# Twelve array splits per pair of heads instead of eighteen, and output sums shared by two pairs

## The chip, the cores and the metric

The kernel runs on one core of a Trainium2 chip. The metric is the device time of one execution in microseconds (us), the median of several runs. The core has TensorE (PE for its matmuls, PEld for its weight loads), VectorE (DVE), ScalarE (ACT), GpSimd (POOL), and SyncE (SP), which here issues most transfers. TensorE's results go to PSUM, which attention uses as eight banks of 128 partitions x 512 float32: four for scores, projections, values and outputs, and four for the products with the values.

TensorE's array can be used whole (128*128 in the profile's rows) or in parts that work side by side: 64*128 is two row groups, 32*64 is four row groups by two column groups. A stretch of matmuls of one such form is called a *split* below.

## The reference, cut to what matters

Four batches of 1024 tokens of width 256 go through causal attention with 16 heads of 64 (rotary positions on queries and keys), a residual sum and a layer norm, then through 16 experts of which each token takes its best 3, and another residual sum and norm. All is float32.

```python
proj = x @ W_in.T + b_in                      # q, k, v of 16 heads
q = _rope(q, sin, cos); k = _rope(k, sin, cos)
att = softmax(where(tril, q @ k.T / 8, -inf))
y = (att @ v) per head
x = layernorm(x + (y @ W_out.T + b_out))
gate = softmax(x @ gate); the best 3, made to sum to 1
x = layernorm(x + sum over the 3 of gate_e * (relu(x @ W1_e + b1_e) @ W2_e + b2_e))
```

## The kernel before, in words

**Pairs of heads.** Attention goes through 32 pairs (4 batches x 8 pairs of heads; two heads fill 128 partitions). The numbers of heads and keys are the same in each pair, and causality makes the work a triangle: a chunk is 128 queries, and query chunk c meets c+1 blocks of 128 keys, c from 7 down to 0.

**The steps of a pair n**, with their functions and lines:
- `project` (L265): queries and keys for 512 tokens at a time (`pp`, L282, 128*128). VectorE reads the bank once (bias, times sine, L287), ScalarE once (bias, L293, `raw`). Four DMAs swap halves of `raw` into `swp` (L305), and `rotate` (L309) on GpSimd multiplies by the cosine and adds (L321, L326). Queries have a lower and an upper half (g = 0 and 1). A pair's projections are made during the pair before.
- `values` (L328): v for two pairs at once (`vv`, L335), copied out by ScalarE (L340), stored to DRAM and read back in another layout by `spread` (L352) into `vr`.
- `scores` (L364): matmuls of 64*128, the two heads side by side (`s`, L385). VectorE takes each bank with a custom reduction (mask, scale, running minimum, L393) and writes `p`; ScalarE then takes exponentials with row sums (L408). `divide` (L419): a reciprocal on VectorE (L422) and a division on GpSimd (L425).
- `turn` (L436): VectorE transposes `p` in 32x32 blocks (L444) into `t_first` (keys 0 to 511) or `t_last` (the others).
- `product` (L451): for key block j the products of 32*64 (L465) with the values, added up over j from 7 to 0 in the four banks `y`, of whose 512 columns they use 256. `close` (L473): ScalarE copies the four banks to `yT` (L479).
- `out` (L486): `yT` times the output weights for 256 tokens (`oo`, L489). VectorE adds the bank to the residual `acc` (L571). Four such blocks per pair.

**Their order.** On TensorE and VectorE the program's order is the written one (L515). A pair is six slots, one per entry of `chunks` (L500): 7, 6, 5, 4, 3 and 2, 1 and 0. Each slot begins with its scores, and the products, projections, outputs and values of the pair before, this one and the next are put between them. In an ordinary pair TensorE thereby goes scores, whole array, products, scores, whole array, products and so on, with 18 splits. The other engines' order comes from a scheduler that follows the program's; `after` adds an order between two instructions, `late` keeps a DMA's place. Instructions of one engine run in their order, so one that waits holds up all behind it.

**The router.** When a batch of attention is done, `batch_done` (L250) makes a list of small steps (norm, transposes, logits, the best three, places) whose planned costs are written beside them. `fill` (L229) puts steps of one engine into the attention loop up to a budget in us; on VectorE 0.7, 2.2, 0.8 and 0.6 per pair. `scatter` (L246) issues the rows' scatters to the experts' buffer from GpSimd (L803), 24 per batch, four per pair. Then comes the experts' stage (`moe`, L951), with the last batch's router beside it.

## Time and profile before

| what | before |
|---|---|
| median of 3 runs | 1581.33 us (1580.61 to 1582.21) |
| the profiled execution | 1580.36 us, its span 1578.5 |
| first 60 us | TensorE busy 49.76 |
| an ordinary pair | 33.75 us, TensorE busy throughout |
| product of key block 0 of pairs 1, 30, 32 | begin at 68.26, 1068.91, 1122.12 us |
| last output of attention | ends at 1129.5 us |
| last matmul of the experts | ends before 1560 us |
| VectorE's additions of outputs (L571) | 128, of 0.66 us each |
| score reductions (L393) | 768 |
| transposes (L444), 128x512 | 384 of 0.68 to 0.69 us |

How to read what follows. A page line of an engine gives its busy time, its share of the span and its number of instructions. The clock line gives, in 40 slices, the granted clock of TensorE in tenths (9 is 0.9 or more). The chain of work that ended last gives pieces with their start and length, where a piece ends as the next begins. A timeline line gives start, length from start to end, engine, line, operation, and tiles written and read; square brackets hold the idle time before it and who ended that. VectorE's instructions overlap by some 0.07 us, so two in a row take less than the sum of their lengths: their steps are counted from start to start. A matmul of 128x512 float32 appears as two records of one pass each.

### The profile page before, as it was taken

To read this page: it belongs to the slowest core of one execution; us is meant where nothing else is said; L and a number is where in the kernel's file an instruction comes from. 1 tells how busy PE (TensorE), PEld (TensorE's weight loads), DVE (VectorE), ACT (ScalarE), POOL (GpSimd) and SP (SyncE) were. 2 spreads that over 40 slices of the span, in tenths; PEclk is the share of its full clock that TensorE was granted. 3 is DMA by queue.
4 is the path that set the end of the run, shared out by engine and by line. 5 is a ranking of instruction groups with operands and counts; after the bars stand their busy time and mean duration, and the time that the engine had idled before them with its cause. 6 is when DMAs were issued, how large, how long until landed. Compare 5 with 4: busy or idle time off the path is not lost.

```text
span 1578.5 us, 52463 instructions
## 1 busy us (share of the span) xinstructions
PE 1502.1 (95%) x20832; PEld 1047.0 (66%) x20832; DVE 1171.5 (74%) x3675; ACT 730.8 (46%) x1694; POOL 979.2 (62%) x928
## 2 busy tenths in 40 slices
PE   7999999999999999999999999999898999999970
PEld 4566666666666666666665666665687888888860
DVE  4888888898899999878999999889756333333324
ACT  3555555556555555655555557554431222222214
POOL 3775665775565677767766766678277843434435
PEclk9999999999999999999999999999999999999985
DMA  6464445546444554564465445545598998989866
GB/s 197 136 161 130 129 128 144 151 129 186 117 121 129 146 145 132 147 193 132 134 174 141 132 132 155 165 120 144 180 315 268 364 273 227 262 246 272 244 187 220
DMA packets 120041, 280.34 MB, mean 178 GB/s; under 512 B 21344, under 2 KB 64608, under 8 KB 108256
## 3 DMA queue, kind: packets, MB, share of 16 engines
q1 hardware_dynamic: 99872, 250.05, 52.9%
q0 software_dynamic: 19584, 26.62, 8.0%
q8 instruction: 166, 2.72, 0.8%
q14 instruction: 83, 0.68, 0.1%
q10 hardware_dynamic: 336, 0.27, 0.1%
HBM read 186.81 MB, written 61.09 MB: 157 GB/s over the span
## 4 chain that ended last, share of the span: by engine, by line
PE 86%; DVE 6%; issue 3%; DMA 3%; POOL 1%; ACT 1%; SPq 0%; ACTq 0%; POOLq 0%; DVEq 0%
PE y_ps L465 18%; PE s L385 17%; PE pp L282 14%; PE ps L1089 10%; PE ps L1073 10%; PE oo L489 7%; PE vv L335 7%; PE ps L1037 1%; DVE t_first L444 1%; DVE p L393 1%; PE lg_ps L706 1%; DMA sums<-y,ids 1%; DVE o_stats L1209 1%; POOL xs L803 1%; DMA vr<-v_d 1%
## 5 line engine op out<-in xcount | busy, mean ns | idle before, releaser
L425 POOL TENSOR_SCALAR p<-p,rinv 128x512 f32<-128x512 f32 (+7 forms) x512 | 374.6, 746 | 336.7 <-DVE rinv L422 291.9
L408 ACT ACTIVATE p<-p,nmax 128x512 f32<-128x512 f32 (+7 forms) x512 | 391.7, 766 | 411.9 <-DVE nmax L393 410.0
L385 PE MATMUL s<-rotk,rotq 64*128 64x512 f32 (+3 forms) x1536 | 309.6, 514 | 2.6 <-DVE rotk L318 2.0
L393 DVE CUSTOM_DVE_ANT_0 p<-s,mask 128x512 f32<-128x512 f32 (+3 forms) x512 | 224.2, 485 | 82.2 <-PE s L385 82.0
L444 DVE STREAM_TRANSPOSE t_first<-p 128x512 f32<-128x512 f32 (+3 forms) x512 | 276.1, 583 | 8.9 <-PE y_ps L465 8.8
L1104 POOL DMA_INDIRECT sums<-y,ids x104 | 163.5, 1572 | 181.1 <-DVE y L1100 121.3
L282 PE MATMUL pp<-xT,wqk 128*128 128x512 f32 x512 | 251.4, 614 | 9.2 <-DMA wqk<-in_w_qk_dram 5.5
L1078 ACT ACTIVATE hid<-ps,w 128x256 f32<-128x256 f32 (+1 forms) x224 | 89.7, 456 | 296.8 <-issue 244.3
L465 PE MATMUL y_ps<-t_first,vr 32*64 32x160 f32 (+2 forms) x8192 | 209.9, 338 | 4.3 <-DVE t_first L444 2.2
L465 PEld LDWEIGHTS y_ps<-t_first,vr 32*64 32x64 f32 x8192 | 165.9, 130 | 58.5 <-issue 44.2
L385 PEld LDWEIGHTS s<-rotk,rotq 64*128 64x128 f32 x1536 | 139.2, 186 | 97.7 <-issue 53.7
L1073 PE MATMUL ps<-xg,w 128*128 128x256 f32 (+1 forms) x896 | 191.7, 367 | 6.8 <-DVE xg L1040 6.8
L1094 DVE TENSOR_TENSOR y<-ps,w 128x512 f32<-128x512 f32 (+1 forms) x56 | 36.6, 653 | 212.9 <-PE ps L1089 175.4
L1089 PE MATMUL ps<-w,hid 128*128 128x256 f32 x832 | 188.8, 379 | 0.5 <-ACT hid L1078 0.5
L393 DVE CUSTOM_DVE_ANT_0 p<-s,zero,nmax 128x512 f32<-128x512 f32 x256 | 181.9, 748 | 2.9 <-PE s L385 0.7
L1073 PEld LDWEIGHTS ps<-xg,w 128*128 128x128 f32 x896 | 158.7, 192 | 25.5 <-DVE xg L1040 7.6
L282 PEld LDWEIGHTS pp<-xT,wqk 128*128 128x128 f32 x512 | 90.0, 190 | 126.1 <-issue 63.0
L1089 PEld LDWEIGHTS ps<-w,hid 128*128 128x128 f32 x832 | 157.2, 190 | 21.6 <-ACT hid L1078 0.7
L465 PEld LDWEIGHTS y_ps<-t_last,vr 32*64 32x64 f32 x7424 | 105.1, 130 | 76.5 <-issue 50.0
L489 PE MATMUL oo<-wo,yT 128*128 128x256 f32 x512 | 141.0, 398 | 2.6 <-ACT yT L479 1.4
L465 PE MATMUL y_ps<-t_last,vr 32*64 32x96 f32 (+3 forms) x7424 | 126.9, 248 | 0.5 <-DVE t_last L444 0.4
L803 POOL DMA_INDIRECT xs<-acc,slots x96 | 97.2, 1012 | 43.9 <-issue 21.8
(187 smaller groups left out, 1726.9 us busy)
## 6 DMA issues: line engine op xcount, KB each, us to landing
w<-in_wall_dram SPq DMA_DIRECT2D x56, 1154.0 KB
vr<-v_d SPq DMA_DIRECT2D x256, 128.0 KB
vr<-v_d SPq DMA_DIRECT2D x128, 256.0 KB
swq<-rawq SPq DMA_DIRECT2D x256, 64.0 KB
v_d<-v SPq DMA_DIRECT2D x128, 128.0 KB
swk<-rawk SPq DMA_DIRECT2D x124, 128.0 KB
x<-xs SPq DMA_DIRECT2D x48, 264.0 KB
wqk<-in_w_qk_dram SPq DMA_DIRECT2D x32, 256.0 KB
```

What stands on the lines that cost most here:

```text
L282: nc.tensor.matmul(ps, lhsT=wqk[n][:, c, i, :], rhs=xts[b, g][:, c, :], start=(c == 0), stop=(c == DC - 1),)
L385: nc.tensor.matmul(s[:, :n_k], lhsT=rot[n, 0, qc // 4][ts(hh, KD), ts(qc % 4, P)], rhs=k[ts(hh, KD), ds(k0, n_k)], start=True, stop=True,)
L393: i = nc.vector.tensor_tensor_reduce(out=probs[n, qc, hh][:, ds(k0, n_k)], in0=s[:, :n_k], in1=mask[:, 512 - n_k :] if diag else zero[:, : ...
L408: order["exp"] = nc.scalar.activation(pr, pr, AF.Exp, bias=m, scale=-1.0, accum_out=rsum[:, hh : hh + 1])
L425: order["divide"] = router.behind = nc.gpsimd.tensor_scalar(pr, pr, rinv[:, hh : hh + 1], 1.0, ALU.mult, ALU.mult)
L444: order["turn"] = router.on_dve = after(nc.vector.transpose(turned[n][h][:, hh, :, ds(i - 4 * h, n_j, step=7 - 4 * h), :], probs[n, i, hh] ...
L465: nc.tensor.matmul(st[n][a][ts(hh, KD), ds(32 * j, 32 * (TC - j))], lhsT=v[ts(a, 32), c * 8 + 2 * u + jh % 2, ts(hh, KD)], rhs=t[ts(a, 32) ...
L489: nc.tensor.matmul(ps[:, v, :], lhsT=st[n][:, ts(2 * h + v, P)], rhs=wo[n], start=True, stop=True,)
L803: i = nc.gpsimd.indirect_dma_start(out=self.xs, out_offset=bass.IndirectOffsetOnAxis(ap=st["slots"][:, r, c : c + 1], axis=0), in_=acc[:, ...
L1073: nc.tensor.matmul(ps[:, f - f0, :], lhsT=w[:, ds(c * FF + f * P, P)], rhs=xg[:, c, :n], start=(c == 0), stop=(c == DC - 1),)
L1089: nc.tensor.matmul(ps[:, h, :], lhsT=hid[:, f, ts(h, P)], rhs=w[:, ds(W2_AT + f * D, D)], start=(f == 0), stop=(f == FC - 1),)
L1104: s = behind(nc.gpsimd.indirect_dma_start(out=sums_of(t), out_offset=bass.IndirectOffsetOnAxis(ap=ids[:, h : h + 1], axis=0), in_=y[:, h, ...
```

## The change

The loop of six slots is replaced by four stretches written out one by one, in which work of one split stands together:
- **Order on TensorE** for pair n: scores 7; a key projection and an output; scores 6; products 4 and 3 of pair n-1; a key projection; products 2, 1, 0 of n-1; scores 5; a query projection; product 7; scores 4, 3, 1, 0, 2; values, a query projection, outputs, values; products 6 and 5. That is 12 splits.
- **Banks.** The lump of scores 4 to 0 needs more than four banks: the tail of chunk 4 and all of chunks 1 and 0 go into the unused half of the four banks `y` (`bank`). `scores` is divided into `multiply` (matmuls) and `scores` (reductions); the order of reductions is 4, 3, 2, 1, 0.
- **Exponentials** can be held back (`hold`) and let go behind a projection's read or a copy of values on ScalarE (`release`).
- **Outputs.** `out` takes two pairs, whose products are added up in one bank, so there is one VectorE addition for two pairs (`plan`, `add`); 68 additions instead of 128. `yT` has three buffers.
- **Swaps.** Keys are swapped in halves of 512 as queries are, so there are 8 swap DMAs of keys per pair instead of 4; `swq` has one buffer, `rotq` for the lower half one.
- **Router.** VectorE's budget per pair is 2.4, before scores 5, and in the first two pairs of a batch 2.0 and 1.4 at the pair's end. Scatters are 1 per pair at its start and 2 behind the reductions of the lump. `x2T`, `hots` and `mine` share one tile `wide`.
- **Buffers.** Each chunk's `p` has its own tiles, `mask` and `zero` are one tile, `v` has two buffers, `xT` of the upper half one.

The core of the diff:

```diff
+        def bank(n, qc, hh, k0):
+            y = st.get(n)
+            if qc == 4 and k0:
+                return y[2 + hh][:, 3 * P :], False
+            if qc == 1:
+                return y[hh][:, 2 * P :], False
+            if qc == 0:
+                return y[2 + hh][:, 2 * P : 3 * P], False
+            return ps_s.tile([P, 512], FP, tag="s", name="s"), True
...
-        def out(n, h):
+        def out(pairs, h):
             ps = ps_s.tile([P, 2, D], FP, tag="s", name="oo")
             for v in range(2):
-                nc.tensor.matmul(
-                    ps[:, v, :], lhsT=st[n][:, ts(2 * h + v, P)], rhs=wo[n],
-                    start=True, stop=True,
-                )
+                for n in pairs:
+                    nc.tensor.matmul(
+                        ps[:, v, :], lhsT=st[n][:, ts(2 * h + v, P)], rhs=wo[n],
+                        start=(n == pairs[0]), stop=(n == pairs[-1]),
+                    )
...
+                if here:
+                    ends = scores(n, (7,), multiply(n, (7,)), hold)
+                    release(1)
+                if before:
+                    divide(n - 1, ends10, last)
+                if ahead and n > 0:
+                    project(n + 1, 1, 0, last)
+                release(behind="raw")
+                last = turns(n - 1, [(3, 0)], last)
+                for o in outs.get((n, 0), []):
+                    parts.append(out(*o))
+                    if n != n_pairs:
+                        last = add(parts.pop(0), last)
+                if here:
+                    divide(n, ends, last)
...
+                    ends = scores(n, (6,), multiply(n, (6,)))
+                for j in (4, 3) if before else ():
+                    product(n - 1, j)
+                last = turns(n - 1, [(2, 0), (1, 0), (0, 0)], last)
+                if ahead:
+                    project(n + 1, 1, 1, last)
+                    fill(PE, 1.0)
...
+                    divide(n, ends, last)
...
+                for j in (2, 1, 0) if before else ():
+                    product(n - 1, j)
+                if before:
+                    close(n - 1)
...
+                last = turns(n, [(7, 1)], last)
+                if n <= n_pairs:
+                    fill(DVE, 2.4, port=0.6)
...
+                    ends5 = scores(n, (5,), multiply(n, (5,)), hold)
+                    release(1)
+                last = turns(n, [(7, 0)], last)
+                if ahead:
+                    project(n + 1, 0, 1, last)
+                release(behind="raw")
+                if here:
+                    product(n, 7)
...
+                    ends4 = scores(n, (4,), multiply(n, (4,)))
+                    p3 = multiply(n, (3,))
+                    small = multiply(n, (1, 0))
+                    ends32 = scores(n, (3, 2), p3 + multiply(n, (2,)), hold)
+                    if before:
+                        scatter(2)
+                    divide(n, ends5, "scores")
+                    ends10 = scores(n, (1, 0), small, hold)
+                    release(2)
+                if vals:
+                    values(m, vals[0])
+                release(2, "v" if vals else None)
+                last = turns(n, [(6, 1)], last)
+                if here:
+                    divide(n, ends4, last)
+                if ahead:
+                    rotate(n + 1, 0, 1)
+                last = turns(n, [(5, 1)], last)
+                if ahead:
+                    project(n + 1, 0, 0, last)
...
+                product_out()
...
+                last = turns(n, [(4, 1)], last)
+                if here:
+                    divide(n, ends32, last)
...
+                last = turns(n, [(6, 0)], last)
+                if vals:
+                    values(m, vals[1])
+                release(8, "v" if vals else None)
+                last = turns(n, [(5, 0), (4, 0)], last)
+                if ahead:
+                    rotate(n + 1, 0, 0)
...
+                if here:
+                    for j in (6, 5):
+                        product(n, j)
+                if p < 2:
+                    fill(DVE, 2.0 - 0.6 * p)
```

## The prediction

> **What bounds the kernel now.** I read the busy shares first, then one ordinary pair of heads in the stretches, then the chain that ended last inside that pair, then VectorE's timeline beside it.
>
> The first two fences are the page's busy line and its line of the granted clock, and one stretch of 33.75 us: a whole pair, from one product of column 0 to the next (columns PE, PEld, DVE, ACT, POOL, granted clock, DMA share, GB/s).
>
> ```profile
> PE 1502.1 (95%) x20832; PEld 1047.0 (66%) x20832; DVE 1171.5 (74%) x3675; ACT 730.8 (46%) x1694; POOL 979.2 (62%) x928
> ...
> PEclk9999999999999999999999999999999999999985
> ```
>
> ```profile
> 101.95:135.70 33.75, 33.75 (x586) 21.17 (x585) 29.14 (x89) 18.18 (x44) 21.36 (x22) 1.00 0.44 119
> ```
>
> In a pair TensorE is busy for all of 33.75 us at a full clock, while VectorE works 29.14, GpSimd 21.36 and ScalarE 18.18. So a pair takes what TensorE's blocks take. The product of column 0 comes at 68.26 us for the first pair and at 1068.91 for the thirtieth: of those 29 periods, most are 33.70 to 33.85, and those with router work are up to 38.8.
>
> The next lines are the chain within one pair (start, length, what). The start of a piece is the end of the one before, so a length holds everything up to the next block.
>
> ```profile
> 600.07 1.12 PE oo L489 x4
> 601.19 1.72 PE pp L282 x4
> 602.91 2.23 PE y_ps L465 x126
> 605.14 1.70 PE s L385 x8
> 606.84 1.91 PE pp L282 x4
> 608.75 3.00 PE y_ps L465 x128
> 611.75 1.49 PE s L385 x8
> 613.25 1.91 PE pp L282 x4
> 615.16 1.91 PE y_ps L465 x64
> 617.07 1.38 PE s L385 x8
> ...
> 627.30 0.85 PE s L385 x8
> 628.15 1.91 PE pp L282 x4
> 630.06 0.86 PE oo L489 x4
> ```
>
> The reader is to compare equal work with different neighbours. A projection right behind an output block (both use the array as 128*128) takes 1.72; between scores (64*128) and products (32*64) it takes 1.91. An output block behind a projection takes 0.86, behind products or scores 1.06 to 1.12. Scores of 7, 6 and 3 key blocks take 1.70, 1.49 and 0.85: 0.213 per block and 0.21 left over. So **each change of the array's split costs some 0.21 us**, wherever it stands. Cross-check: 4 projections at 1.72, 4 outputs at 0.86, 2 value blocks at 1.73, 36 score blocks at 0.213, and products at 0.214 per 32 columns (8+7+6+5+4 units; the short ones, 1.94 in all, by their pieces less 0.2) make 29.9 us; 33.75 less that is 3.8 us, over 18 splits 0.21.
>
> **The change, part by part.**
>
> *Splits.* The order on TensorE is written out by hand, so it can be counted in the built programs: 572 changes of split before, 382 after, 18 and 12 in an ordinary pair. 190 x 0.21 = **39.9 us less**. The boundary step alone is smaller (the last step of scores before a projection is 0.52 where it is 0.42 inside, so 0.10), the other half shows as one late second matmul behind it. If only the first half goes, the gain is 19 us; that is the lower bound. I take the whole, because it comes out of four kinds of block alike.
>
> *Shared sums.* TensorE multiplies as much as before (two pairs' outputs go into one bank, four matmuls for two). VectorE's additions fall from 128 to 68; one costs 0.58 us from its start to the next, so a pair loses 1.15 us: 29.14 becomes 28.0. TensorE sets the end, so this alone is worth nothing; it pays for the next item.
>
> *Scores in a lump.* Scores of chunks 4, 3, 1, 0 and 2 now stand together, with banks for the small ones in the unused columns of the products' four banks. VectorE must drain them while the 4 score banks turn over. The next lines are its timeline (start, length, what).
>
> ```profile
> 520.30 0.69 DVE L393 CUSTOM_DVE_ANT_0 p<-s,mask 128x512 f32<-128x512 f32 x1 [0.33 <-PE s L385]
> ...
> 520.92 0.69 DVE L393 CUSTOM_DVE_ANT_0 p<-s,mask 128x512 f32<-128x512 f32 x1
> ...
> 521.53 0.55 DVE L393 CUSTOM_DVE_ANT_0 p<-s,mask 128x384 f32<-128x384 f32 x1
> ```
>
> Steps count from start to start: 0.61 for a masked 512, 0.67 for an unmasked, 0.48, 0.34 and 0.21 for 384, 256 and 128; transposes 0.62, 0.49, 0.365 and 0.19; a projection's read 0.65. I walk one pair with these, time 0 at the scores of chunk 5, 0.2 per split, data ready some 0.2 behind a block's stream.
>
> TensorE: scores 5 to 1.3, projection 1.5 to 3.2, product 7 to 3.9, the lump 4.1 to 7.3, values to 9.3, projection to 11.0, a shared output (now 1.73) to 12.7, values to 14.5, products 6 and 5 to 16.1, scores 7 from 16.3 to 18.1, projection from 18.25, output to 21.7, scores 6 to 23.5, products 4 and 3 to 25.8, projection to 27.7, products 2 to 0 to 32.4.
>
> VectorE: scores 5 and two transposes to 4.05, projection 4.7, scores 4 6.6, scores 3 7.9, scores 2 8.8, scores 1 and 0 10.0, four transposes 11.8, projection 12.4, two transposes and a sum 13.5, six transposes 17.2, scores 7 17.35 to 19.9, projection 20.8, two transposes 22.0, sum 22.6, scores 6 to 25.0, and then it idles until scores 5.
>
> Three places are tight. Scores 2 need the banks of scores 4, free at 6.7 when TensorE is at 6.65. The projection behind scores 7 needs their first bank, free at 18.0, and is there at 18.25. The last quarter of scores 6 needs the bank of the shared output, free at 22.66, and is there at 22.54. So about 0.1 us of waiting per pair by the walk; I charge 0.2 for the spread of VectorE's rows: 31 x 0.2 = **6 us back**. VectorE idles 4 us beside products 2 to 0, so lag does not carry into the next pair, and the router's work for it (2.4 us planned there) is covered.
>
> *Router.* Where a batch has just ended, up to 2.0 or 1.4 us of the router's VectorE work now stand right before scores 7, where there is no slack: three batches, about 1.4 each, **4 us back** (0 to 6). Its TensorE blocks stay beside projections and outputs, at no split.
>
> *Softmax exponentials moved behind projection reads and value copies.* ScalarE works 18.18 of 33.75 us and each exponential still lies 2 us or more ahead of its reciprocal in the walk; nothing, or up to 0.3 us per pair if the copy of values comes late.
>
> *Swaps for rotation.* The key halves are swapped one by one: 4 more DMA issues of about 0.6 us on SP, whose queue then also waits for the single swap buffer (until GpSimd has rotated the upper query half, 15.2 in the walk). The next keys land by about 31, are rotated by about 37 and are used at 49; nothing. The upper half's rotation (2 x 1.28 on GpSimd) stands behind the divisions of chunks 5 and 4, ends at 15.2 and is needed at 16.3: 1.1 us of cover, and each us over it costs a us per pair.
>
> *Scatters* (1.0 us each on GpSimd, 3 instead of 4 per pair) stand behind the division of chunk 6, where GpSimd waits for the key swap. *Rows left for the experts' stage* are the same 24 in both programs, and the router's last lists close at the same place. Its 450 us I take as unchanged (up to 3 us either way, as its first weights wait for other tiles).
>
> Sum against the profiled execution (1580.36 us, its span 1578.5): -39.9 + 6 + 4 = -30, so 1550.4; the median of the runs is 1.0 above it, so **1551 us**.
>
> **A rule that speaks against it.** VectorE worked 29.14 of 33.75 us in the stretch shown. The Trainium skill, page "TensorEngine Tiling (Array Packing)", section "PSUM Bottleneck", says that tiling speeds up TensorE and not the emptying of PSUM, which may then become the limit. If VectorE set the pair and kept all its 4.6 us of idle time, the pair would lose just its two sums: 32.6 us, and the sum would be 31 x 1.15 = 36 us less, 1546; by the row, TensorE still sets it.
>
> **The rivals.**
>
> *VectorE is partly late* (0.17). If its lump takes 0.5 to 0.9 us longer than walked (3 to 5% of the 17 us from scores 5 to scores 7), the projection behind scores 7 and the last quarter of scores 6 wait about as long: 31 x 0.4 to 0.8 = 12 to 25 us, 1563 to 1576. For it: three margins below 0.3 us. Against it: the steps come from rows with GpSimd running beside.
>
> *VectorE is fully late, and the kernel slower* (0.10). Place: TensorE waits at the projection behind scores 7 and at the weights of scores 7, since the reciprocal of chunk 4, the division behind it and the upper rotation come late too. Price: a us per pair for each us beyond 0.2. It decides from 1.2 us on, where 31 x 1.0 eats the 30 us; at 2 us it gives 1551 + 31 x 1.8 = 1607.
>
> *Half the split cost stays* (0.07): -19 + 10 = -9, 1572.
>
> *No waits at all* (in the forecast's case): -39.9 and nothing back, 1541, less a little from the start, 1538.
>
> That the change does not do what it says is excluded by the built order.
>
> **How the numbers follow.** Forecast 0.66 (1538 to 1562), partly late 0.17 (to 1576), half cost 0.07 (about 1572), fully late 0.10 (1580 to 1610). The range reaches from 1538 to 1576 and leaves out the last case and some edges. Faster by over 0.2% (below 1578, about what a measurement of this kernel can tell from no change) 0.88, within 0.2% 0.04, slower 0.08.
>
> **What would show it.** Right: a steady pair of 32.4 to 32.8 us in stretches with TensorE busy throughout; a projection of about 1.9 with a split on each side, as before; VectorE near 28.0 us per pair, idle mostly before scores 5. Wrong: idle time on TensorE, or longer pieces of projection or scores 6, ended by VectorE's reads; scores 7 waiting for rotq; a pair above 33; or score and product blocks that grow as their neighbours go.

## The result, and the profile after

The changed kernel takes **1595.84 us** (median of 4 runs, 1593.63 to 1597.49) beside 1581.77 (4 runs, 1580.61 to 1584.02) of the kernel before on the same chip: 1.0086 times as long, with an interval of 1.0069 to 1.0104. It is slower; 1551 was forecast. Its profiled execution took 1596.47 us, with a span of 1594.6.

The page's lines of busy time and granted clock, after:

```profile
PE 1504.7 (94%) x20832; PEld 1079.6 (68%) x20832; DVE 1149.1 (72%) x3615; ACT 723.3 (45%) x1694; POOL 980.4 (61%) x927
...
PEclk9999999999999999999999999999999999999995
```

TensorE does the same 20832 matmuls, and the clock line looks the same; VectorE has 60 instructions less. Nothing here tells of a slower kernel. The stretches of two ordinary pairs, one behind the other, tell more:

```profile
199.97:233.56 33.59, 33.59 (x609) 22.29 (x601) 28.26 (x86) 17.94 (x42) 21.71 (x23) 1.00 0.49 128
233.56:266.80 33.24, 33.24 (x570) 21.48 (x563) 28.26 (x86) 17.95 (x42) 20.70 (x23) 1.00 0.52 144
```

VectorE fell from 29.14 to 28.26, about as forecast (28.0), but the pair is 33.24 to 33.59 and not 32.4 to 32.8. TensorE still counts as busy throughout, because a matmul that waits for its bank inside a block is hidden in the block's length. So the blocks have to be compared with their own work. TensorE's timeline of the first of these pairs (start, length):

```profile
206.23 0.49 PE L384 MATMUL y_ps<-rotk,rotq 64*128 64x128 f32 x4
...
209.47 0.81 PE L384 MATMUL s<-rotk,rotq 64*128 64x384 f32 x2
210.21 1.99 PE L330 MATMUL vv<-wv,xT 128*128 128x256 f32 x8
...
224.52 2.10 PE L384 MATMUL s<-rotk,rotq 64*128 64x384 f32 x8
226.55 1.19 PE L485 MATMUL y_ps<-t_last,vr 32*64 32x128 f32 x63
...
230.69 5.38 PE L485 MATMUL y_ps<-t_first,vr 32*64 32x192 f32 x192
236.01 1.56 PE L384 MATMUL s<-rotk,rotq 64*128 64x256 f32 x8
```

Counted from start to start, scores 6 take 2.03 us (224.52 to 226.55) where seven blocks at 0.213 and a split make 1.70: 0.32 too much. Scores 4 to 0 begin at 206.23 and last to 210.21, 3.98 where their columns and a split make 3.42: 0.56. Products 2 to 0 take 5.31 where they take 4.73 in the next pair. In the same way I went through all blocks between the first and the last product of key block 0 (68.26 to 1121.85 us before, 68.06 to 1138.43 after), with a split at 0.205 us:

| | before | after |
|---|---|---|
| from the first to the last of these products | 1053.6 us | 1070.4 us |
| the blocks' work, by their columns | 904.3 | 908.7 |
| splits, at 0.205 us each | 550: 112.8 | 365: 74.8 |
| beyond work and split, in scores | 12.1 | 45.2 |
| the same, in products | 15.3 | 26.6 |
| the same, in projections, values, outputs | 9.2 | 14.8 |

The work is the same, so its 4 us of difference show how far such sums can be trusted (matmul records that a trace lacks). **The splits' 38 us are gained and 50 us beyond work and splits are new**, 17.2 of the scores' 45.2 in scores 4 to 0, 15.4 in scores 6, 8.0 in scores 7.

By pairs (pair k is the k-th period from one product of key block 0 to the next): against 29 periods of 33.75, the kernel before spends 21.9 us more, in the pairs with router work. Against 29 of 33.26 the changed one spends 48.0 more. So ordinary pairs gave 29 x 0.49 = 14.2 us, the borders of the batches took back 26, the last two periods 4.9. The 26 us lie in pairs 8, 9, 16, 17, 24 and 25, where one batch gives way to the next: these six take 225.9 us, and six ordinary pairs would take 199.6.

Not all of the 50 us is waiting. Between 68 and 1122 us the kernel before has a granted clock of 1.0 throughout. The changed kernel has it at 0.5 in three stretches, of 6.83 us from 582.9 (pair 16), of 3.41 from 893.5 (pair 24) and of 3.41 from 1132.4. The first one as a stretch (the clock is the third number from the end):

```profile
582.90:589.70 6.80, 4.42 (x38) 1.88 (x40) 5.83 (x12) 1.03 (x2) 4.13 (x2) 0.50 0.24 76
```

Just ahead of it TensorE had stood still for 4.44 us (from 580.8). It is busy for 10.5 us in the three stretches together; half of that, some 5 us, is an estimate of what the clock costs here.

### The profile page after: what moved, and what is told of

Same layout as the page of the kernel before. It is cut to its first block, busy times and chain, and to the rows that moved or that the text cites. A ratio compares the mean times of both kernels' runs of the same rounds, so it can differ in the third digit from the quotient of the medians.

```text
span 1594.6 us, 52381 instructions
## 1 busy us (share of the span) xinstructions
PE 1504.7 (94%) x20832; PEld 1079.6 (68%) x20832; DVE 1149.1 (72%) x3615; ACT 723.3 (45%) x1694; POOL 980.4 (61%) x927
## 4 chain that ended last, share of the span: by engine, by line
PE 84%; DVE 6%; POOL 3%; DMA 3%; issue 3%; ACT 1%; SPq 0%; ACTq 0%; POOLq 0%; DVEq 0%
PE y_ps L485 18%; PE s L384 15%; PE pp L287 14%; PE ps L1171 10%; PE ps L1187 10%; PE oo L510 6%; PE vv L330 6%; PE y_ps L384 2%; DVE p L403 1%; PE ps L1135 1%; DMA sums<-y,ids 1%; POOL p L445 1%; PE lg_ps L802 1%; DVE t_first L464 1%; DVE o_stats L1307 1%
## 5 line engine op out<-in xcount | busy, mean ns | idle before, releaser
L384 PE MATMUL s<-rotk,rotq 64*128 64x512 f32 (+2 forms) x1152 | 304.6, 567 | 7.8 <-POOL rotq L321 3.0
L287 PE MATMUL pp<-xT,wqk 128*128 128x512 f32 x512 | 255.9, 624 | 19.4 <-DVE nmax L403 14.0
L464 DVE STREAM_TRANSPOSE t_first<-p 128x512 f32<-128x512 f32 (+3 forms) x512 | 266.4, 577 | 0.0
L403 DVE CUSTOM_DVE_ANT_0 p<-s,mask 128x512 f32<-128x512 f32 (+2 forms) x320 | 170.7, 578 | 96.0 <-PE s L384 91.0
L485 PE MATMUL y_ps<-t_first,vr 32*64 32x160 f32 (+3 forms) x8192 | 206.5, 338 | 3.6 <-issue 2.1
L485 PEld LDWEIGHTS y_ps<-t_first,vr 32*64 32x64 f32 x8192 | 175.4, 131 | 35.3 <-DVE t_first L464 22.4
L403 DVE CUSTOM_DVE_ANT_0 p<-s,mask,nmax 128x512 f32<-128x512 f32 x256 | 181.8, 747 | 8.4 <-PE s L384 5.9
L384 PEld LDWEIGHTS s<-rotk,rotq 64*128 64x128 f32 x1152 | 125.8, 186 | 91.7 <-issue 44.1
L298 ACT ACTIVATE raw<-pp,bqk 128x512 f32<-128x512 f32 x128 | 87.9, 687 | 146.0 <-issue 98.3
L464 DVE STREAM_TRANSPOSE t_last<-p 128x512 f32<-128x512 f32 (+3 forms) x256 | 116.9, 489 | 13.7 <-POOL p L445 13.5
```

The costliest lines, as they stand in the source:

```text
L287: nc.tensor.matmul(ps, lhsT=wqk[n][:, c, i, :], rhs=xts[b, g][:, c, :], start=(c == 0), stop=(c == DC - 1),)
L384: nc.tensor.matmul(s[:, :n_k], lhsT=rot[n, 0, qc // 4][ts(hh, KD), ts(qc % 4, P)], rhs=k[ts(hh, KD), ds(k0, n_k)], start=own, stop=True, s ...
L403: i = nc.vector.tensor_tensor_reduce(out=probs[n, qc, hh][:, ds(k0, n_k)], in0=s[:, :n_k], in1=mask[:, 512 + P - n_k :] if diag else zero[ ...
L464: order["turn"] = router.on_dve = after(nc.vector.transpose(turned[n][h][:, hh, :, ds(i - 4 * h, n_j, step=7 - 4 * h), :], probs[n, i, hh] ...
L485: nc.tensor.matmul(st[n][a][ts(hh, KD), ds(32 * j, 32 * (TC - j))], lhsT=v[ts(a, 32), c * 8 + 2 * u + jh % 2, ts(hh, KD)], rhs=t[ts(a, 32) ...
```

## The experiments

The experiments ran on four chips. On two of them the kernel before takes 1600 us, on the others 1581, so times are compared only with the kernel before on the same chip.

**Is it the bank that scores 3 wait for?** (before: 1599.64 us in this group of four)

```diff
-                last = turns(n, [(7, 0)], last)
+                if here:
+                    turn(n, 7, 0, 0, last)
+                    last = "turn"
...
+                if here:
+                    turn(n, 7, 1, 0, last)
+                    last = "turn"
```

> The changed kernel, with the second head's transpose of chunk 7's lower half moved behind the reductions of the lump, so that VectorE reads the query projection some 0.6 us earlier. Theory A (the lump waits because the projection's bank, which scores 3 take over, is held until ScalarE has read it too, and ScalarE reads only after VectorE): an ordinary pair goes from 33.26 to 32.8-32.95 us and the run gets 9 to 15 us shorter than the changed kernel. Rival B (VectorE is full from scores 5 to scores 7, and what is taken out in one place comes back at scores 7): the pair stays within 0.1 of 33.26 and the run within 3 us.

Measured: 1640.1 us, 1.0262 (1.0235 to 1.0290), ordinary pairs 33.37 instead of 33.26. Scores 4 to 0 lost half of their wait (0.56 to 0.29), but scores 7 waited 0.38 anew, and the pair did not gain. One line each of ScalarE and VectorE in the lump that begins at 207.26:

```profile
207.55 0.69 ACT L298 ACTIVATE raw<-pp,bqk 128x512 f32<-128x512 f32 x1 [0.87 <-ACT p L418]
```

```profile
209.32 0.75 DVE L403 CUSTOM_DVE_ANT_0 p<-s,mask,nmax 128x512 f32<-128x512 f32 x1
```

The two heads' matmuls of a block begin within 0.01 us of each other when both have their banks. In the changed kernel scores 3 do not: the first head begins at 207.42, the second, which takes over the projection's bank, at 207.86, just behind the end of ScalarE's read of that bank (207.12 + 0.69 = 207.81). Here that read ends at 208.24, and both heads begin together at 208.44. So this wait was for ScalarE's read, and it is gone. What is left of the lump's wait stands one block further on: the second head of scores 2 begins at 210.13 and the first at 209.95, because VectorE reads scores 4's bank until 210.07. The wait was only passed on, to the next bank and to scores 7, and both times VectorE is the one that is late.

**Two edits at the batch border.** The residual's additions on GpSimd moved to the second pair; the key rotation put behind scores 5.

```diff
-                if n == 1 or p == 0 and 0 < b < B:
+                if p == 1 and b < B:
                     residual(b, 0)
...
-                if n == 1 or p == 0 and 0 < b < B:
+                if p == 1 and b < B:
                     residual(b, 1)
```

> The changed kernel, with GpSimd's two additions of the bias to the residual made in the second pair of a batch instead of the first. Theory A (in the first pair of a batch they stand on GpSimd beside the router's VectorE steps, which wait for them, and in the last batch they wait for the residual's load and hold up the divisions behind them): the pairs that took 43.5 and 44.4 us come to 37 to 39 (they hold four shared outputs, 3.5 us more than an ordinary pair), the run gets 9 to 13 us shorter. Rival B (VectorE is full there anyway): both pairs stay above 41 and the run within 4 us.

Measured: 1619.33 us, 1.0118 (1.0083 to 1.0153). Pair 16 fell from 43.53 in the change's first profile to 37.2, pair 24 from 44.39 to 40.41, pair 8 from 37.44 to 36.84. (The kernel with the transposes moved, on the same chip as this one and with the additions where they were, has 44.02, 44.19 and 37.59.) The 6.83 us of half clock in pair 16 are gone too. VectorE's timeline at pair 16, first in the changed kernel, then in this one, shows why:

```profile
576.61 1.12 DVE L94 TENSOR_TENSOR tot<-pr,tot 128x128 f32<-128x128 f32 x1
...
578.67 1.06 DVE L94 TENSOR_TENSOR tot<-tot,shift 128x128 f32<-128x128 f32 x1
579.65 2.31 DVE L94 TENSOR_TENSOR at<-pr,shift 128x16 f32<-128x16 f32 x1
...
582.30 2.59 DVE L94 TENSOR_TENSOR wide<-wide,slot 128x384 f32<-128x384 f32 x1
```

```profile
576.74 0.28 DVE L94 TENSOR_TENSOR tot<-pr,tot 128x128 f32<-128x128 f32 x1
...
578.09 0.17 DVE L94 TENSOR_TENSOR at<-pr,shift 128x16 f32<-128x16 f32 x1
...
578.63 0.56 DVE L94 TENSOR_TENSOR wide<-wide,slot 128x384 f32<-128x384 f32 x1
```

The six steps take 8.3 us (576.61 to 584.89) and 2.5 (576.74 to 579.19). GpSimd's timeline in the changed kernel beside them:

```profile
577.56 2.03 POOL L445 TENSOR_SCALAR p<-p,rinv 128x896 f32<-128x896 f32 x2
579.56 2.37 POOL L209 TENSOR_TENSOR acc<-acc,bo 128x1024 f32<-128x1024 f32 x1
581.90 2.58 POOL L316 TENSOR_TENSOR swk<-swk,cos 128x1024 f32<-128x1024 f32 x1
```

VectorE's step from 579.65 ends at 581.96, when the addition that began ahead of it ends (581.93); the one from 582.30 ends at 584.89, beside the rotation's end (584.48). The step from 578.67 ends at 579.73, beside the end of the two divisions (579.59). A VectorE step that reads two tiles from SBUF stood still until the GpSimd step that had begun ahead of it was done. The Trainium skill, page "SBUF — State Buffer", section "SBUF: two separate sides", states it: such a VectorE operation and a GpSimd operation share a pair of ports as an exclusive lock, and the second one waits for the whole of the first. A 16-column step of 0.17 that takes 2.31 us agrees.

> The changed kernel, with the rotation of the keys on GpSimd made to wait for the reductions of scores 5, so that it no longer runs beside the router's VectorE steps; GpSimd then ends it at 8 instead of 6.2 us after scores 5, before the division that needs GpSimd at 9.3. Theory A (a VectorE step that reads and writes SBUF waits until GpSimd's running addition ends): no router step longer than 1.3 us beside a rotation, the pair of 43.5 loses 2 to 3 us, the run gets 2 to 6 us shorter. Rival B (the steps' number, not the collision): no step but those already short changes, the run within 2 us. A loss of over 2 us would say that the rotation has less cover than thought.

Its edit makes the rotation's first step wait for the reductions of scores 5 and puts it behind them in the program:

```diff
+            if i:
+                tc.add_manual_dep(
+                    first.ins, order["scores"].ins.name, SYNC, reason="behind the scores"
+                )
...
-                if ahead:
-                    rotate(n + 1, 1)
...
+                if ahead:
+                    rotate(n + 1, 1)
```

Measured: 1635.02 us, 1.0234 (1.0204 to 1.0263); pair 16 at 43.02, pair 24 at 46.63, ordinary 33.26. With the additions still there, the six steps of pair 16 take 6.6 us (577.12 to 583.69) instead of 8.3: the rotation's part is the last step, 0.56 instead of 2.59. In pair 24 the late rotation stands from 894.39 to 899.16 ahead of the divisions of chunk 5, and TensorE waits 4.82 us behind them; the pair is 2.2 us longer than in the change's first profile.

**What is one split worth in the old order?** Twice one split was taken out of the kernel before.

```diff
-                    if k in (3, 4) and here:
-                        product(n, 10 - k)
+                    if k == 4 and here:
+                        product(n, 7)
+                        product(n, 6)
```

> The kernel before, with product 7 made together with product 6, one slot later: one change of the array's split less in each of the 32 pairs and nothing else moved. A split costs 0.21 us: the ordinary pair goes from 33.75 to 33.54, the run gets 6 to 7 us shorter than before. If half of it stays: 33.65 and 3 us. If the split's price is a wait in disguise: no gain.

Measured: 1610.65 us, 1.0075 (1.0048 to 1.0101), ordinary pairs 34.01. TensorE's timeline, this kernel and then the one before:

```profile
205.69 1.45 PE L385 MATMUL s<-rotk,rotq 64*128 64x128 f32 x8
207.54 1.10 PE L489 MATMUL oo<-wo,yT 128*128 128x256 f32 x4 [0.40 <-ACT yT L479]
```

```profile
205.05 1.46 PE L385 MATMUL s<-rotk,rotq 64*128 64x128 f32 x8
206.44 0.73 PE L465 MATMUL y_ps<-t_last,vr 32*64 32x32 f32 x40
207.09 1.13 PE L489 MATMUL oo<-wo,yT 128*128 128x256 f32 x4
```

Product 7 shrank from 0.66 us, start to start, to 0.47 where it stands with product 6: the split is worth 0.19 (0.21 was forecast). But the output block behind the scores now waits 0.40 for ScalarE's copy of the pair's output, and the scores' block grew from 1.39 to 1.85. Product 7 had been the time in which that copy was made.

The second one moved product 0 up to products 2 and 1 (before: 1581.11 us in this group of three):

```diff
-                    if k == 2 and before:
-                        product(n - 1, 0)
-                        close(n - 1)
...
+                    if k == 1 and before:
+                        product(n - 1, 0)
+                        close(n - 1)
```

> The kernel before with one edit: the product of key block 0 (and the copies of its output) moves up to products 2 and 1, so that 192 small matmuls follow one another and scores 4 follow the projection directly; one array split less in each pair. Price theory (a split costs 0.2 us wherever it is taken out): an ordinary pair goes from 33.75 to 33.55. Supply theory (a run of 192 small matmuls outlasts TensorE's stock of instructions): the 0.2 are gained, but in about every second pair the run shows 0.3 to 0.6 us of excess with no engine or transfer named as what it waits for, as in the changed kernel, so that pairs alternate, 33.6 and 33.9 to 34.1. Cover theory (a product between two blocks of scores gives VectorE its time): scores 4 or what follows them wait, some 0.3 to 0.8 us in every pair alike, as where products 7 and 6 were joined in the kernel before, and the pair is 33.8 to 34.3.

Measured: **1667.85 us, 1.0547** (1.0529 to 1.0565), ordinary pairs 35.4 to 37.1. None of the three theories had the size, but the place is the one that the cover theory named. TensorE's timeline:

```profile
207.11 4.80 PE L465 MATMUL y_ps<-t_first,vr 32*64 32x192 f32 x192
211.83 1.56 PE L385 MATMUL s<-rotk,rotq 64*128 64x256 f32 x8
213.32 1.98 PE L282 MATMUL pp<-xT,wqk 128*128 128x512 f32 x4
215.24 1.35 PE L385 MATMUL s<-rotk,rotq 64*128 64x128 f32 x6
217.48 1.12 PE L385 MATMUL s<-rotk,rotq 64*128 64x512 f32 x2 [0.90 <-ACT rawq L293]
218.53 0.70 PE L465 MATMUL y_ps<-t_last,vr 32*64 32x32 f32 x40
219.16 1.55 PE L489 MATMUL oo<-wo,yT 128*128 128x256 f32 x4
220.51 3.20 PE L335 MATMUL vv<-wv,xT 128*128 128x256 f32 x8
```

Scores 4 stand 1.9 us closer to scores 5 than before. VectorE is not through with scores 5, two transposes and the projection's bank by then, and ScalarE, which reads that bank second, frees it at about 217.4. Scores 4 take 3.29 us instead of 1.39; that is the bank. The outputs and values behind them are slow too, the values 3.13 us instead of 1.82, and that is not the bank. It is the granted clock (third number from the end):

```profile
219.70:223.10 3.40, 3.40 (x10) 2.68 (x9) 2.93 (x8) 1.19 (x4) 3.32 (x3) 0.50 0.18 43
```

In these 3.41 us the matmuls of the values begin 0.43 us apart, and 0.216 otherwise. TensorE stands still for 0.9 us or more in each of the first 30 pairs, at scores 4, and behind 20 of these waits the clock is at 0.5 for 3.41 us (once for 6.83). The pairs of 35.4 us have no such stretch, those of 37.1 have one; why it follows some of the waits and not the others is not shown. **A product between two blocks of scores is not only a split of 0.2 us, it is the time in which VectorE and ScalarE empty the banks**; a split saved there cost 1.7 us per pair in waiting, and another 1.7 in the pairs where the clock fell behind the wait. The long run of 192 products itself showed its plain 4.73 us in most pairs.

**Scatters, borders, VectorE's load** (before: 1600.42 us in this group of four). First the changed kernel itself:

> The changed kernel itself, unaltered, so that the others of this call have it beside them on one chip. Both theories expect a ratio of 1.01 to 1.03 to the kernel before, an ordinary pair of 33.2 to 33.4 us in its first half, and pairs 16 and 24 at 43 to 45 us. The scatter theory (GpSimd's indirect DMAs beside products of key blocks make TensorE issue them slowly) expects the ordinary pairs after 600 us at 34 to 36 us on a chip where the kernel before also shows it, and that most of that excess lies in products that run within 0.2 us of an indirect DMA; the theory that VectorE is simply full expects the same 33.3 us there as in the first half.

Measured: 1630.2 us, 1.0177 (1.0148 to 1.0206): twice the loss on the result's chip. Its first half is the known one (ordinary 33.26 to 33.53), pairs 16 and 24 take 44.6 and 41.7, but after 600 us ordinary pairs take 35.2 to 36.1. That is where the scatters begin.

```diff
                     if before:
+                        router.behind = order["rotated"]
                         scatter(2)
```

> The changed kernel with the two scatters that follow scores 3 and 2 put behind the next pair's key rotation in GpSimd's queue instead of ahead of it, so that they run beside scores 4 to 0 and the values and not beside the product of key block 0; nothing else moves. Scatter theory: the pairs after 600 us fall by 1 to 2.5 us each where they are slow, 10 to 30 us in all on a chip that shows it (4 us on one that does not). VectorE-full theory: no change, within 3 us of the changed kernel; or slower by up to 0.5 us per pair, because the key rotation is now earlier and GpSimd's next division, 2 us of scatters later, is behind.

Measured: 1605.58 us, 1.0036 (1.0021 to 1.0052), **24.6 us less**; ordinary pairs are 33.2 to 33.6 again after 600 us. TensorE's line of products 2 to 0 and GpSimd's scatters in the changed kernel:

```profile
768.41 7.00 PE L485 MATMUL y_ps<-t_first,vr 32*64 32x192 f32 x192
```

```profile
771.59 1.06 POOL L901 DMA_INDIRECT xs<-acc,slots  x1 [0.16 <-issue]
772.95 0.98 POOL L901 DMA_INDIRECT xs<-acc,slots  x1 [0.30 <-issue]
```

and the same two views with the scatters behind the key rotation:

```profile
759.23 4.80 PE L485 MATMUL y_ps<-t_first,vr 32*64 32x192 f32 x192
```

```profile
768.18 2.37 POOL L321 TENSOR_TENSOR rotk<-rotk,swk 128x1024 f32<-128x1024 f32 x1
770.70 1.06 POOL L902 DMA_INDIRECT xs<-acc,slots  x1 [0.15 <-issue]
```

The 192 matmuls take 2.2 us more beside two scatters. The wait has no releaser: the trace names neither an engine nor a transfer, only slow issue. All products between 605 and 1100 us, PE's busy time (the two kernels in turn):

```profile
605.00:1100.00 495.00, 155.40 (x6600) 119.45 (x6600) 1.00 0.51 138
```

```profile
605.00:1100.00 495.00, 137.19 (x6825) 117.93 (x6807) 0.99 0.51 142
```

More matmuls in 18 us less. By runs of products 2 to 0 between 605 and 1100 us: here all 13 with scatters beside them take 2.0 to 2.5 us more than 4.73, 29 in all; with the scatters moved, 9 of 14 take the plain 4.73. On the result's chip the same kernel's 14 runs beside scatters take 0 to 1.1 us more, 4.4 in all. The two scatters were meant to stand with the lump of scores, but GpSimd comes to them only behind the division of chunk 6, and there they run beside products 2 to 0. In the kernel before the two ran 31 us after the start of product 0, beside scores 5.

```diff
-                    scatter(1)
+                    scatter(2)
...
-                if n == 1 or p == 0 and 0 < b < B:
+                if p == 1 and b < B:
                     residual(b, 0)
...
-                if n == 1 or p == 0 and 0 < b < B:
+                if p == 1 and b < B:
                     residual(b, 1)
...
+                        router.behind = order["rotated"]
                         scatter(2)
```

> As the one with the scatters behind the key rotation, and besides both halves of the residual's addition move to the second pair of a batch, and two scatters instead of one go at a pair's start, so that a batch's rows are out in six pairs and the next residual's load is not held. Border theory (router steps on VectorE end when GpSimd's two-input steps end, and the late load holds the divisions): pair 16 falls from 43.5 to 37 us, pair 24 from 44.4 to 36 to 38, pair 8 by 0.6; 15 to 20 us in all beyond the scatters' own gain, and the kernel comes out at 0.985 to 0.995 of the kernel before. VectorE-full theory: the router's work only moves, the sum of the pairs falls by under 6 us, and the ratio to the kernel before stays above 1.

Measured: **1589.01 us, 0.9937** (0.9906 to 0.9968). Pair 16 takes 37.86, pair 24 38.48 (51.16 with the scatters' move alone), pair 8 36.82. In the changed kernel pair 24 stood like this on GpSimd:

```profile
874.47 4.66 POOL L209 TENSOR_TENSOR acc<-acc,bo 128x1024 f32<-128x1024 f32 x2 [3.38 <-DMA acc<-in_x_dram]
879.10 3.34 POOL L445 TENSOR_SCALAR p<-p,rinv 128x768 f32<-128x768 f32 x4
```

Three scatters a pair instead of four end batch 0's rows at 865 us, the last batch's residual is loaded only then (867.33, before 843.54), GpSimd waits for it, and the divisions of chunk 5 wait behind. With four a pair this is gone.

> The changed kernel without VectorE's additions of the shared output products to the residual (four of 0.65 us for two pairs, 1.3 us per pair), which leaves the attention's output out of what follows; TensorE's products stay. Bank theory (TensorE waits only where one bank is still unread): the last quarter of scores 6 no longer waits for an output's bank, 0.32 us of an ordinary pair's 33.26 go, and a little of the rest, 32.7 to 33.0 in all. VectorE-full theory: the pair falls by what VectorE lost, 1.3 us, to 32.0. A third, that neither matters and TensorE's instructions come late in the long runs of products: 33.2, unchanged.

```diff
         def add(part, last):
-            a, ps = part
-            order["sum"] = after(nc.vector.tensor_tensor(a, ps, a, ALU.add), last)
-            router.on_dve = order["sum"]
-            return "sum"
+            return last
```

Measured: ordinary pairs mostly 32.96 to 33.05, 0.3 less. (Its whole time, 1655.99, says nothing here: without the sums the router sends other tokens to the experts.) TensorE's line of scores 6:

```profile
224.43 1.77 PE L384 MATMUL s<-rotk,rotq 64*128 64x384 f32 x8
226.13 1.19 PE L485 MATMUL y_ps<-t_last,vr 32*64 32x128 f32 x63
```

1.70 from start to start instead of 2.03, so the 0.32 of scores 6 were the shared output's bank. VectorE lost 1.3 us of work per pair and the pair 0.3: VectorE is not full. It is late at certain places and idle at others.

**Can VectorE's work be placed better?** Two kernels built on the one with the mended borders, in the group with 1581.11 us.

```diff
-                    fill(DVE, 2.4, port=0.6)
+                    fill(DVE, 4.0, port=0.6)
...
-                if p < 2:
-                    fill(DVE, 2.0 - 0.6 * p)
```

> The kernel with scatters, residual and load mended, and with the router's VectorE steps all in the idle time ahead of scores 5 (4.0 us of them in a pair, instead of 2.4 there and 2.0 or 1.4 at the end of the first two pairs of a batch). Border theory (the fill at the end of a pair stands in front of the reductions of scores 7, which TensorE's projection waits for): pairs 9, 17 and 25 lose the 1 to 1.5 us that scores 7 show in them and the 1.9 us of scores 6, some 2 to 4 us per batch and 6 to 10 in all, 0.985 to 0.991 of the kernel before. VectorE-full theory: the steps cost what they take wherever they stand, 4.0 us now end after scores 5 are there, and the sum stays within 3 us, 0.992 to 0.996.

Measured: **1571.38 us, 0.9935** (0.9918 to 0.9952), the best of this study. Pairs 9, 17 and 25 take 31.4, 31.8 and 31.1 instead of 33.2, 33.0 and 33.7, as the border theory had it, but the ratio lies where the VectorE-full theory had it. These pairs hold no output block (the pairs ahead of them hold four), so they should take some 29.8, an ordinary pair's 33.26 less two shared outputs of 1.73. The six border pairs take 207.7 us here, 213.0 in the kernel that this one builds on and 225.9 in the changed kernel. That kernel ran on another chip, one on which the kernel before itself loses time, so how much of the ratio this edit gives is not measured. Nor does most of the gain over the kernel before come from attention: from the last product 0 to the end it is 449.4 us here and 456.7 before. The router's `wide` steps, one per batch, stand in pairs 14, 22 and 30 here; before, they stood in 16 and 25, the third behind the last product 0. TensorE waits 0.5 us for the first gathered rows instead of 4.6, and no stretch of half clock follows (6.83 us before). Between the first and the last product 0 it is 1050.5 us instead of 1053.6.

```diff
-                last = turns(n, [(7, 1)], last)
+                last = turns(n, [(7, 1), (6, 1)], last)
...
-                last = turns(n, [(7, 0)], last)
+                if here:
+                    turn(n, 7, 0, 0, last)
+                    last = "turn"
...
-                last = turns(n, [(6, 1)], last)
+                if here:
+                    turn(n, 7, 1, 0, last)
+                    last = "turn"
```

> The kernel with scatters, residual and load mended, and with 1.1 us of VectorE's transposes (chunk 6, upper half) moved from behind the reductions of scores 3 to 0 into the idle time ahead of scores 5, and the second head's transpose of chunk 7's lower half (0.6 us) moved from ahead of scores 4's reductions to behind those of scores 0. Placement theory (VectorE has 8 us of idle time in a pair, but between scores 5 and products 6 and 5 it is always the one that is late): the wait in scores 4 to 0 falls from 0.56 to 0.3 us as in the run where only the second move was made, and this time scores 7 do not pay for it; an ordinary pair is 32.9 to 33.1, 5 to 10 us in all. VectorE-full theory, or theory that the banks' order and not VectorE sets that wait: 33.25 to 33.4.

Measured: 1576.7 us, 0.9974 (0.9963 to 0.9985), ordinary pairs 32.98. TensorE's timeline at scores 4 to 0:

```profile
205.39 0.49 PE L384 MATMUL y_ps<-rotk,rotq 64*128 64x128 f32 x4
...
209.10 1.99 PE L330 MATMUL vv<-wv,xT 128*128 128x256 f32 x8
```

3.71 instead of 3.98, and scores 7 do not pay. VectorE has the same work, in another place, and the pair 0.28 us less. The last of attention's products 0 begins at 1118.4 here and at 1119.9 in the kernel before this one; the whole is 5 us longer because the experts' stage is, where TensorE waits 3.3 us for the first gathered rows instead of 0.5, and where its clock is at 0.5 for 3.41 us from 1138.1 and 6.83 from 1189.3, which makes some 5 us more.

Both together (before: 1581.63 us):

> The two kernels of the last call put together: transposes moved as in the one, and the router's VectorE steps ahead of scores 5 alone as in the other, 3.2 us of them in a pair because 1.1 us of transposes now stand there too. If both gains are what they were read as, waits of different places, they add up: ordinary pairs 32.9 to 33.1, pairs 9, 17 and 25 at 31 to 33, and 0.985 to 0.991 of the kernel before. If they draw on the same idle time of VectorE ahead of scores 5, the second gain is lost again as lateness of scores 5: 0.992 to 0.998.

Measured: 1583.6 us, 1.0018 (1.0000 to 1.0035). Ordinary pairs keep 32.98 to 33.01, but eight pairs instead of six are above 36 us. The new ones are pairs 17 (40.2) and 25 (39.05), whose scores 5 wait 4.9 and 4.0 us. GpSimd, VectorE and TensorE in pair 17:

```profile
610.58 2.36 POOL L209 TENSOR_TENSOR acc<-acc,bo 128x1024 f32<-128x1024 f32 x1
```

```profile
611.15 1.82 DVE L94 TENSOR_TENSOR at<-pr,shift 128x16 f32<-128x16 f32 x1
...
613.30 2.63 DVE L94 TENSOR_TENSOR wide<-wide,slot 128x384 f32<-128x384 f32 x1
```

```profile
619.20 3.78 PE L287 MATMUL pp<-xT,wqk 128*128 128x512 f32 x4 [4.82 <-DVE nmax L403]
```

The two edits draw on the same 4 us of VectorE ahead of scores 5. With 3.2 us a pair the router's steps come into the second pair of a batch, to which the residual's additions had been moved, and the collision is back. Behind TensorE's wait the clock is at 0.5 for 10.24 us in each of the two pairs.

## Why the prediction was wrong

*The price of a split held.* 185 splits fewer between the first and last product 0 at 0.205 us are 38 us (39.9 were forecast for 190), and a single one, taken out by itself, gave 0.19. (The cross-check's terms make 29.8 and not 29.9, which changes nothing.) Two terms that take time back were too small, and they make most of the miss of 45 us: 29 ordinary pairs gave 14 us where the forecast's 1.03 each makes 30, the borders took 26 where 4 were forecast, and the last two periods lost 4.9 where 2 were to be gained. Why those two lost was not followed.

*"I charge 0.2 for the spread of VectorE's rows: 31 x 0.2 = 6 us back"* is the first step that failed. The pair of before shown in the prediction has 0.3 us beyond work and splits; an ordinary changed pair of 33.26 has 1.0. Of the 1.23 us of six splits, 0.49 were left: some 0.7 us per pair came back, not 0.2. Of the three tight places, scores 6 waited 0.32 (0.12 by the walk), shown by the run without the sums. Scores 4 to 0 waited 0.56 (0 by the walk): the walk counted the projection's bank as free once VectorE had read it (207.04 in the trace), but ScalarE reads it after that. VectorE's and ScalarE's lines:

```profile
206.33 0.71 DVE L292 SCALAR_TENSOR_TENSOR rotq<-pp,bqk,sin 128x512 f32<-128x512 f32 x1
```

```profile
207.12 0.69 ACT L298 ACTIVATE raw<-pp,bqk 128x512 f32<-128x512 f32 x1 [1.46 <-issue]
```

That read ends at 207.81, and the second head of scores 3 begins in that bank at 207.86, 0.44 us behind the first head. Where the read ended before the bank was needed, the two heads began together and the wait fell to 0.29, which was then VectorE's, one bank further on. So the walk's mistake is the bank's second reader, shown by the run with the transposes moved. The third place, the projection behind scores 7, held in ordinary pairs.

*"About 1.4 each, 4 us back (0 to 6)" for the router* is the second: the borders cost 26 us. In this term the fill ahead of scores 7 was indeed dear (pairs 9, 17 and 25 fell by 1.2 to 2.6 us without it), but two things were missing. The residual's additions were not mentioned, and they were moved into the very 4 us that the text called cover: six router steps took 8.3 us there instead of 2.5, and TensorE's wait behind them was followed by 6.83 us at half clock, which no term of the sum foresaw. And "3 instead of 4" scatters a pair was costed at nothing, without asking who waits for the last one: the last batch's load.

*Scatters "stand behind the division of chunk 6"*: right, and that puts them beside products 2 to 0. On the result's chip this costs some 4 us, on another 24.6. The trace of before could not show it, since few of its products lay beside scatters.

*The rivals.* "VectorE partly late" had the mechanism, with 0.4 to 0.8 us a pair and up to 1576; with the borders' 22 us beyond the forecast it would have been close, though it does not name them. "VectorE fully late" had the sign and a range that holds 1596, but not the reason: 1.3 us less on VectorE gave 0.3, and lateness is gone by scores 5, ahead of which VectorE idles. The rule that the prediction quoted against itself came true bank by bank (0.32 and 0.56 us a pair), and not for VectorE's sum. "Half the split cost stays" is refuted. VectorE at 28.0 us (28.26) and an unchanged experts' stage (456.7 and 456.2 us from the last product 0 to the end) held.

**What stays open.** Products 2 to 0 take 0.3 to 1.1 us beyond their 4.73 in every second or third pair, 7 us in all, with no releaser; 4.4 of the 7 lie in pairs with scatters beside them, the rest in pairs without. The same run in the old order mostly did not, so its length alone is not the cause. Why scatters slow these products, and more on some chips than on others, is open as well.

## What to carry to other kernels

A block of small matmuls between two blocks that fill PSUM is cover: before joining blocks to save a split, walk each bank to its last reader, and count the removed block's time as time that the reader loses. What was moved out of the way is to be followed on its own queue, with the question what shares its port and who waits for the last of it. A busy engine in a stretch is no proof that it works: compare each block with its columns, and look at the granted clock before calling a long block a wait.

## What the runs showed of the hardware

Products of 32*64 slow down beside GpSimd's indirect DMAs: 192 of them take 6.9 us instead of 4.73 beside two scatters on one chip (13 of 13 runs 2.0 to 2.5 us longer), and on the result's chip 0 to 1.1 us longer. Scores and whole-array matmuls beside scatters showed nothing of the kind: in the run with the scatters moved, their steps from start to start beside scatters and elsewhere are within 3% of each other.

VectorE's steps with two SBUF inputs, of 0.2 to 0.6 us, last 2.3 to 2.6 us when GpSimd has begun a two-input step of 2.4 us ahead of them, and one of 0.3 lasts 1.06 beside a division of 1.0.

TensorE's granted clock was 0.5 for stretches of 3.41, 6.83 or 10.24 us behind waits of TensorE: behind 20 of 30 waits of 0.9 to 1.5 us in the kernel with product 0 moved up, and behind one of 4.44 us at a batch's border in the changed kernel.
